# An own order for the head, the latent output and the handover to the experts, with a pool that is given up early

## The chip, the cores and the metric

The kernel runs on one core of a Trainium2 chip. The metric is the device time of one execution in microseconds (us). The engines are called as in the profile: PE (TensorE, matmul and transposes; PEld is its weight load), DVE (VectorE), ACT (ScalarE), POOL (GpSimd) and SP (SyncE, which issues most DMAs). Everything is in float32.

## What is computed

It is one decoder layer for 32 sequences of 256 tokens with 256 channels: causal self-attention with 16 heads on a shared latent of 72 numbers, cross-attention to 120 context rows, a mixture of 16 experts with a fixed capacity beside one shared expert, and a layernorm after each. Cut to what matters:

```python
Wdkv = x @ latent_w + latent_b                      # 72 columns, for all heads
q = einsum('btc,hcl->bhtl', x, Wd_w) + Wd_b
attn = softmax(causal(q @ Wdkv.T / sqrt(d_head)))
x = layernorm(x + reshape(attn @ Wdkv) @ out_w + out_b)
q, k, v = x @ Wq, ctx @ Wk, ctx @ Wv                # 16 heads of 64
x = layernorm(x + (softmax(q * depth**-0.5 @ k.T) @ v) @ Wo)
scores = softmax(x @ gate_w.T)                      # each expert takes its best 32 tokens of a sequence
flat = scatter_add(zeros, idx, (gelu(x_tok @ Wg) * (x_tok @ Wu)) @ Wd * score)
x = layernorm(x + flat + shared_expert(x))
```

## The kernel before, in words

The attention of a sequence n is cut into four quarters of four heads each. `attention_round(n)` (L795) runs them, each beginning with `scores(n, g)` (L401, called S0 to S3 here). Around them stands work of older sequences, so that PE always has something to do while a softmax is on its way: sequence n-1 gets its latent output and its cross queries, n-2 its cross softmax and output, n-3 is transposed and routed. `run` drops a step whose sequence doesn't exist, `both` runs a cross step for two column groups, `turns` the three transposes of a quarter.

The order within this section is written by hand for PE and ACT (`manual_schedule`). DVE, POOL and SP are ordered by the compiler's scheduler, which puts what stands under `urgent()` ahead; in the setup all engines go in program order, SP also in round 0. In the expert section PE and POOL are in program order.

The steps that matter here, with the names that the profile shows:

- `load` (L309) fetches x; `turn_x` (L320) transposes it (pxT, copied to xT on DVE, L174); `keys` (L327) projects to pk, from which ACT makes kT and DVE kD; `query_rest` (L361) and `queries` (L373) project the queries (pq) with wd_sb, a reordered copy of wd_w that `order_weights` (L254) makes: two DVE copies for the small rest (L266), one DVE copy `pack` for the first quarter (L260), the others on POOL, and scaled biases wdbs (L276).
- `scores` (L401) fills four PSUM banks (pS); DVE adds the mask and makes sm (L432). `weights` and `softmax` (L435, L442): DVE takes the maximum (nmax, L445), ACT the exponentials with their sums (L448), DVE the reciprocal (rs, L455), POOL the product (L456). `turn` (L458) transposes the result (pT) and copies it (pt, on ACT or DVE). `weigh` (pz, L490) and `weigh_rest` (pzr, L511) apply it.
- `latent_out` (L521): 36 matmuls to po, DVE adds the residual (r, L531), and `layernorm` (L143) makes x1: two statistics and two aggregates on DVE, an addition to rstd, its power -1/2 on POOL (L154), and two DVE instructions that write x1 (L156). `turn_x1` (L535) transposes x1 (px1T), copied on DVE (x1T).
- `cross_queries` (pqx), `cross_keys` (pkx), `cross_values` (pvx), `cross_scores` (pL), `cross_weights` (softmax to xsm_x), `cross_turn` (pxT at L623), `cross_weigh` (pc), `cross_out` (po at L653 and on, then layernorm 2); `turn_x2` (L671) transposes x2 (px2T).
- After round 31 comes `last_section` (L888). Then the self-attention pools are closed, and the expert pools take their place. `feed_forward` (L1062) is a generator of stretches; `fill(k)` (L1088) runs the next k, between which the last cross-attention steps are written by hand. `Expert.load` (L948) issues three weight loads on SP and four gathers on POOL (L958, xe), `turn` transposes the rows (px, L967), `gated` makes pg and pu, `down` pd and four scatters on POOL, which add into acc (L995).

PSUM has six banks for the tag r, and two for the tag l.

Of the kernel before, what the change touches and what calls it, by code (L numbers as in the profile page):

```python
# [26 lines left out]
P = 128  # L27
# [5 lines left out]
def decoder_kernel(  # L33
# [85 lines left out]
    nc.gpsimd.memset(mhalf, -0.5)  # L119

# [76 lines left out]
    ap = cross_pools.enter_context(tc.tile_pool(name="ca", bufs=2))  # L197
    self_pools = ExitStack()
# [5 lines left out]
    lat_sb = wp.tile([P, DC, LW], F32, name="lat_sb")  # L204
# [4 lines left out]
    wd_sb = wp.tile([P, DC, H * L], F32, name="wd_sb")  # L209
# [4 lines left out]
    wk_sb = cw.tile([P, DC, H * DH], F32, name="wk_sb")  # L214
    wv_sb = cw.tile([P, DC, H * DH], F32, name="wv_sb")
# [6 lines left out]
    kr = wp.tile([P, NG, T], F32, name="kr")  # L222
# [5 lines left out]

    def first_weights():


        raw = ow_sb.rearrange("p a b -> p (a b)").rearrange("p (c n) -> p c n", c=DC)
        nc.sync.dma_start(
            out=lat_sb[:, :, 0:L], in_=latent_w.rearrange("(c p) l -> p c l", p=P)
        )
        nc.sync.dma_start(out=raw, in_=wd_w.rearrange("(c p) n -> p c n", p=P))
        nc.scalar.dma_start(out=latb[0:L], in_=latent_b.unsqueeze(1))
        for j in range(1, HG):
            nc.scalar.dma_start(
                out=latb[LM + j * LR : LM + (j + 1) * LR], in_=latent_b[LM:].unsqueeze(1)  # L240
            )
        by_column = wd_b[LM:, :].rearrange("l (g j o) -> j (l g) o", j=HG, o=1)
        for j in range(HG):
            nc.sync.dma_start(
                out=wdbs[j * 32 : (j + 1) * 32, ZC - 1 : ZC], in_=by_column[j]
            )
        nc.vector.tensor_copy(
            lat_sb[:, :, L:].rearrange("p c (j l) -> p c j l", l=LR),
            lat_sb[:, :, LM:L].unsqueeze(2).to_broadcast([P, DC, HG - 1, LR]),
        )  # L250
        nc.scalar.dma_start(out=wdb_sb, in_=wd_b)
        nc.sync.dma_start(out=outb, in_=out_b.partition_broadcast(P))

    def order_weights():  # L254
        raw = ow_sb.rearrange("p a b -> p (a b)").rearrange("p (c n) -> p c n", c=DC)
        by_head = raw.rearrange("p c (h l) -> p c h l", l=L)

        def pack(copy, g):
            at = slice(2 * g * P, 2 * (g + 1) * P)
            copy(  # L260
                wd_sb[:, :, at].rearrange("p c (h l) -> p c h l", l=LM),
                by_head[:, :, g * HG : (g + 1) * HG, 0:LM],
            )

        for d in range(DC):
            nc.vector.tensor_copy(  # L266
                wd_sb[:, d, H * LM :].rearrange("p (j l g) -> p j l g", j=HG, l=LR),
                by_head[:, d, :, LM:].rearrange("p (g j) l -> p j l g", j=HG),
            )

        nc.vector.tensor_scalar(
            wdbs[:, ZC - 1 : ZC], wdbs[:, ZC - 1 : ZC], QSCALE, None, ALU.mult
        )
        pack(nc.vector.tensor_copy, 0)
        for odd in range(2):
            nc.vector.tensor_scalar(  # L276
                wdbs[odd * LM : (odd + 1) * LM, 0 : H // 2],
                wdb_sb[0:LM, :].rearrange("l (c two) -> l c two", two=2)[:, :, odd],
                QSCALE,
                None,  # L280
                ALU.mult,
            )
        for g in range(1, NG):
            pack(nc.gpsimd.tensor_copy, g)
# [510 lines left out]
    def attention_round(n):  # L795
        scores(n, 0)
        run(cross_scores, n - 2, 4, 0)
        run(cross_values, n - 1, 0)
        turns(n - 1, 3)
        both(cross_turn, n - 2, 0, 1)  # L800
        weights(n, 0, 0)
        queries(n, 1)
        run(turn_x2, n - 3)
        weights(n, 0, 1)
        run(weigh_rest, n - 1)
        run(weigh, n - 1, 2)
        run(weigh, n - 1, 3)
        if routed(n):
            route((n - 3) // BQ)
        run(cross_weigh, n - 2, 0)  # L810
        both(cross_weights, n - 2, 4, 0)
        run(latent_out, n - 1)
        if n:
            run(load, n + 1)
            run(load_context, n + 1)
        best_of(n, 1)

        scores(n, 1)
        run(cross_scores, n - 2, 4, 1)
        run(cross_values, n - 1, 1)  # L820
        turns(n, 0)
        both(cross_turn, n - 2, 4, 0)
        weights(n, 1, 0)
        cross_keys(n, 0)
        weights(n, 1, 1)
        run(turn_x1, n - 1)
        if n == 0:
            out_weights(0)
        if routed(n):
            score((n - 3) // BQ)  # L830
        queries(n, 2)
        run(cross_weights, n - 2, 4, 1, 0)
        run(cross_queries, n - 1, 0, 0)
        run(cross_weights, n - 2, 4, 1, 1)
        run(cross_queries, n - 1, 0, 2)
        best_of(n, 2)

        scores(n, 2)
        run(cross_scores, n - 1, 0, 0)
        run(cross_queries, n - 1, 4, 0)  # L840
        turns(n, 1)
        both(cross_turn, n - 2, 4, 1)
        weights(n, 2, 0)
        run(turn_x, n + 1)
        run(cross_queries, n - 1, 4, 2)
        weights(n, 2, 1)
        queries(n, 3)
        run(keys, n + 1)
        run(cross_weights, n - 1, 0, 0, 0)
        run(query_rest, n + 1)  # L850
        run(cross_weights, n - 1, 0, 0, 1)
        if n == 0:
            load_weights([(wv_sb, wv)])
            out_weights(1)
        best_of(n, 3)

        weigh(n, 0)
        weigh(n, 1)
        run(cross_weigh, n - 2, 4)
        scores(n, 3)  # L860
        run(cross_scores, n - 1, 0, 1)
        run(queries, n + 1, 0)
        turns(n, 2)
        run(place_keys, n + 1)
        both(cross_turn, n - 1, 0, 0)
        both(cross_weights, n - 1, 0, 1)
        cross_keys(n, 1)
        weights(n, 3, 0)
        run(values, n + 1)
        weights(n, 3, 1)  # L870
        run(cross_out, n - 2)
        if n == 0:
            load_weights([(wq_sb, wq), (wo_sb, wo), (gw_sb[:, :, 0:E], gate_w)])


        if n - 3 >= BG and (n - 3) % BG == 0:
            place((n - 3) // BG - 1)
        if n - 3 >= 0 and (n - 2) % BG == 0:
            select((n - 3) // BG)
# [8 lines left out]
    def last_section():  # L888

        cross_values(last, 0)  # L890
        both(cross_turn, last - 1, 0, 1)
        weigh(last, 2)
        turns(last, 3)
        turn_x2(last - 2)
        weigh(last, 3)
        weigh_rest(last)
        cross_weigh(last - 1, 0)
        cross_scores(last - 1, 4, 0)
        both(cross_weights, last - 1, 4, 0)
        latent_out(last)  # L900

    every = {getattr(mybir.EngineType, n) for n in ("PE", "SP", "DVE", "Activation", "Pool")}
    with tc.manual_schedule(engines=every):
# [6 lines left out]
        order_weights()  # L910
        query_rest(0)
        queries(0, 0)
# [5 lines left out]
    with tc.manual_schedule(engines={*by_hand, mybir.EngineType.SP}):  # L918
        attention_round(0)
    with tc.manual_schedule(engines=by_hand):  # L920
        for n in range(1, B):
            attention_round(n)
        last_section()
    self_pools.close()
# [3 lines left out]
    fw = expert_pools.enter_context(tc.tile_pool(name="fw", bufs=1))  # L928
    fp = expert_pools.enter_context(tc.tile_pool(name="fp", bufs=2))
    wsg_sb = fw.tile([P, DC, F], F32, name="wsg_sb")  # L930
    wsu_sb = fw.tile([P, DC, F], F32, name="wsu_sb")
    wsd_sb = fw.tile([P, FC, C], F32, name="wsd_sb")
# [3 lines left out]
    class Expert:  # L936
# [11 lines left out]
        def load(self):  # L948
            e = self.e
            self.wg = fp.tile([P, DC, F], F32, tag="wg", name=f"wg_{self.nm}")  # L950
            nc.sync.dma_start(out=self.wg, in_=wg[e].rearrange("(c p) f -> p c f", p=P))
            self.wu = fp.tile([P, DC, F], F32, tag="wu", name=f"wu_{self.nm}")
            nc.sync.dma_start(out=self.wu, in_=wu[e].rearrange("(c p) f -> p c f", p=P))
            self.wd = fp.tile([P, FC, C], F32, tag="wd", name=f"wd_{self.nm}")
            nc.sync.dma_start(out=self.wd, in_=wd[e].rearrange("(c p) d -> p c d", p=P))
            self.xe = fp.tile([P, NBK, XW], F32, tag="xe", bufs=3, name=f"xe_{self.nm}")
            for k, b in enumerate(self.blocks):
                nc.gpsimd.indirect_dma_start(  # L958
                    out=self.xe[:, k, :], out_offset=None, in_=xrows[b], in_offset=self.rows(b)
                )  # L960

# [41 lines left out]
    class Shared:  # L1003


        wg, wu, wd = wsg_sb, wsu_sb, wsd_sb

# [4 lines left out]
        def load(self):  # L1012
            if self.pair == 0:
                nc.sync.dma_start(out=wsg_sb, in_=ws_g.rearrange("(c p) f -> p c f", p=P))
                nc.sync.dma_start(out=wsu_sb, in_=ws_u.rearrange("(c p) f -> p c f", p=P))
                nc.sync.dma_start(out=wsd_sb, in_=ws_d.rearrange("(c p) d -> p c d", p=P))
            self.xT = fp.tile([P, DC, cols], F32, tag="xeT", bufs=3, name=f"fx2T_{self.nm}")
            nc.sync.dma_start(out=self.xT, in_=x2ts[self.pair].rearrange("p c i t -> p c (i t)"))

# [42 lines left out]
    def feed_forward():  # L1062
# [5 lines left out]
        units[0].load()  # L1068
        yield
        units[1].load()  # L1070
        units[0].turn()
        yield
        for u, unit in enumerate(units):
# [7 lines left out]
            if u + 2 < len(units):  # L1081
                units[u + 2].load()
            yield
# [8 lines left out]
    with tc.manual_schedule(engines={mybir.EngineType.PE, mybir.EngineType.Pool}):  # L1092
        fill(1)
        cross_values(last, 1)
        cross_scores(last - 1, 4, 1)
        both(cross_weights, last - 1, 4, 1)
        both(cross_turn, last - 1, 4, 0)
        turn_x1(last)
# [98 lines left out]
```

## Time and profile before

| | us |
|---|---|
| median of 3 runs | 3424.97 (3423.62 to 3425.28) |
| profiled execution | 3423.19 |
| its span | 3421.4 |
| busy: PE | 3386.6 |
| busy: DVE, ACT, POOL | 1549.0, 1491.7, 1071.0 |
| PE waiting for the two first causes: POOL's sm, the first x | 5.9, 4.0 |

The profiled execution is one of its own; its span lies between its first and last instruction. A row of the waits says: the engine and the instruction that waited, the engine and the instruction that released it, then the total, how often, and the longest. A row of a timeline says: start, length, engine, line of the code, operation, output and inputs with their shapes, how many in a row, and in brackets the idle time of the engine just before and what ended it. Matmuls overlap, so in a row of several the next may start before the listed end. The granted clock is the share of full speed that PE's clock had. "Steady" is a round in the middle of the first section.

### The profile page before, as it was taken

To read this page: it belongs to the slowest core of one execution; us is meant where nothing else is said; L and a number is where in the kernel's file an instruction comes from. 1 tells how busy PE (TensorE), PEld (TensorE's weight loads), DVE (VectorE), ACT (ScalarE), POOL (GpSimd) and SP (SyncE) were. 2 spreads that over 40 slices of the span, in tenths; PEclk is the share of its full clock that TensorE was granted. 3 is DMA by queue.
4 is the path that set the end of the run, shared out by engine and by line. 5 is a ranking of instruction groups with operands and counts; after the bars stand their busy time and mean duration, and the time that the engine had idled before them with its cause. 6 is when DMAs were issued, how large, how long until landed. Compare 5 with 4: busy or idle time off the path is not lost.

```text
span 3421.4 us, 60519 instructions
## 1 busy us (share of the span) xinstructions
PE 3386.6 (99%) x23516; PEld 2569.9 (75%) x23516; DVE 1549.0 (45%) x3416; ACT 1491.7 (44%) x5458; POOL 1071.0 (31%) x947
## 2 busy tenths in 40 slices
PE   8999999999999999999999999999999999999999
PEld 6888888888888888888888888886666655666555
DVE  4555455555555555545555645553322133222133
ACT  4555555555545655555555555554211111111111
POOL 3333323322323323223323232332444411444400
PEclk9999999999999999999999999999999999999999
DMA  3000000000000000000000000003455532455421
GB/s 98 9 17 23 20 22 17 18 18 23 20 21 18 18 17 23 21 20 19 17 18 17 24 20 21 16 12 100 104 125 125 132 91 59 117 125 124 106 84 50
DMA packets 142614, 164.58 MB, mean 48 GB/s; under 512 B 29432, under 2 KB 118264, under 8 KB 142328
## 3 DMA queue, kind: packets, MB, share of 16 engines
q1 hardware_dynamic: 117536, 126.08, 12.3%
q0 software_dynamic: 24576, 34.62, 5.7%
q8 instruction: 187, 3.06, 0.4%
q14 instruction: 99, 0.81, 0.1%
q10 hardware_dynamic: 216, 0.01, 0.0%
HBM read 105.61 MB, written 50.86 MB: 46 GB/s over the span
## 4 chain that ended last, share of the span: by engine, by line
PE 96%; DVE 2%; ACT 1%; POOL 1%; DMA 0%; issue 0%; SPq 0%; POOLq 0%; DVEq 0%
PE po L180 14%; PE pq L180 7%; PE pqx L180 7%; PE pu L180 6%; PE pd L180 6%; PE pg L180 6%; PE pS L423 5%; PE pz L490 5%; PE pT L470 5%; PE pc L639 3%; PE pkx L180 3%; PE pg_s L180 3%; PE pu_s L180 3%; PE pL L597 3%; PE pfo L180 3%; PE pxT L623 3%
## 5 line engine op out<-in xcount | busy, mean ns | idle before, releaser
L456 POOL TENSOR_TENSOR sm<-sm,rs 128x512 f32<-128x512 f32 (+1 forms) x256 | 375.2, 1466 | 675.6 <-DVE rs L455 624.8
L448 ACT ACTIVATE sm<-sm,nmax 128x128 f32<-128x128 f32 (+1 forms) x1024 | 453.0, 458 | 4.5 <-DVE nmax L445 4.3
L456 POOL TENSOR_TENSOR xsm_x<-xsm_x,rs_x 128x480 f32<-128x480 f32 x256 | 252.4, 986 | 610.9 <-DVE rs_x L455 609.9
L448 ACT ACTIVATE xsm_x<-pL,nmax_x 128x120 f32<-128x120 f32 x1024 | 353.4, 373 | 9.4 <-DVE nmax_x L445 9.4
L995 POOL DMA_INDIRECT acc<-eo,offs x128 | 200.8, 1568 | 322.3 <-DVE eo L992 292.9
L432 DVE TENSOR_TENSOR sm<-pS,mask 128x384 f32<-128x384 f32 x512 | 249.5, 548 | 77.0 <-PE pS L423 76.9
L180 PE MATMUL pq<-xT,wd_sb 128*128 128x256 f32 x1152 | 280.1, 384 | 2.6 <-DVE wd_sb L266 2.6
L566 ACT COPY vx<-pvx 120x512 f32<-120x512 f32 x64 | 37.5, 586 | 509.7 <-PE pvx L180 509.7
L180 PE MATMUL po<-ow_sb,zT 128*128 128x256 f32 x1152 | 257.2, 382 | 0.0
L180 PEld LDWEIGHTS po<-ow_sb,zT 128*128 128x128 f32 x1152 | 216.4, 190 | 39.8 <-DVE cxT L651 8.5
L180 PE MATMUL pu<-xeT,wu 128*128 128x512 f32 x512 | 242.1, 596 | 0.0
L180 PE MATMUL pqx<-x1T,wq_sb 128*128 128x256 f32 x1024 | 241.9, 385 | 0.0
L180 PE MATMUL pg<-xeT,wg 128*128 128x512 f32 x512 | 240.7, 593 | 0.0
L1059 DVE TENSOR_TENSOR hT<-gl,pu 128x512 f32<-128x512 f32 x128 | 87.9, 687 | 334.7 <-PE pu L180 254.6
L180 PEld LDWEIGHTS pq<-xT,wd_sb 128*128 128x128 f32 x1152 | 212.5, 191 | 33.1 <-DVE wd_sb L266 3.4
L445 DVE TENSOR_REDUCE nmax<-sm 128x4 f32<-128x512 f32 (+1 forms) x256 | 231.7, 946 | 3.2
L154 POOL TENSOR_TENSOR rstd<-rstd,mhalf 128x2 f32<-128x2 f32 (+1 forms) x97 | 67.1, 692 | 526.4 <-DVE rstd L153 526.4
L180 PE MATMUL po<-wo_sb,cxT 128*128 128x256 f32 x1024 | 227.6, 381 | 0.0
L180 PE MATMUL pd<-wd,hT 128*128 128x256 f32 x1024 | 226.3, 379 | 0.0
L448 ACT ACTIVATION_READ_ACCUMULATOR xsm_x<-pL,nmax_x 128x1 f32 x1024 | 226.0, 221 | 0.0
L180 PEld LDWEIGHTS pqx<-x1T,wq_sb 128*128 128x128 f32 x1024 | 191.3, 192 | 27.3
L180 PEld LDWEIGHTS pd<-wd,hT 128*128 128x128 f32 x1024 | 192.4, 190 | 25.6 <-issue 1.0
(136 smaller groups left out, 6211.7 us busy)
## 6 DMA issues: line engine op xcount, KB each, us to landing
wg<-in_wg_dram SPq DMA_DIRECT2D x32, 512.0 KB
wu<-in_wu_dram SPq DMA_DIRECT2D x32, 512.0 KB
wd<-in_wd_dram SPq DMA_DIRECT2D x32, 512.0 KB
x<-in_x_dram SPq DMA_DIRECT2D x32, 256.0 KB
rows<-x SPq DMA_DIRECT2D x32, 256.0 KB
acc<-x SPq DMA_DIRECT2D x32, 256.0 KB
x2t<-x2T SPq DMA_DIRECT2D x32, 256.0 KB
fx2T_s<-x2t SPq DMA_DIRECT2D x16, 512.0 KB
```

Source lines behind the costliest of these rows:

```text
L180: nc.tensor.matmul(acc, lhsT, rhs, start=(i == 0), stop=(i == n - 1))
L423: nc.tensor.matmul(pS[2 * a + odd][:, SEG[t]], st["qT", g][rows, a, t * P : (t + 1) * P], k[rows, 0 : (t + 1) * P], start=False, stop=(t = ...
L432: nc.vector.tensor_tensor(sm[:, j, :], pS[j], mask, ALU.add)
L445: nc.vector.tensor_reduce(nmax, src, AX.X, ALU.max, negate=True)
L448: nc.scalar.activation(dst[:, a, :], src[:, a, :], AF.Exp, bias=nmax[:, a : a + 1], accum_out=rs[:, a, :],)
L456: nc.gpsimd.tensor_tensor(dst, dst, rs.to_broadcast([P, n, width]), ALU.mult)
L470: nc.tensor.transpose(pT[:, j, :], block, ident)
L490: nc.tensor.matmul(pz[odd * LM : (odd + 1) * LM, a, k * P :], st["v"][:, k, 0:LM], moving(st, g, 2 * a + odd, k), start=(k == 0), stop=(k ...
L597: nc.tensor.matmul(pLs[odd][:, j, :], st["qxT", c0][rows, j, t * P : (t + 1) * P], st["kxT"][rows, c0 + j, :], start=True, stop=True,)
L623: nc.tensor.transpose(pT[:, j, :], st["xsm", c0, t, odd][:, j, :], ident)
L639: nc.tensor.matmul(pc[odd * DH : (odd + 1) * DH, a, :], st["vx"][:, 2 * (c0 + j0 + a) + odd, :], st["xpt", c0, odd][:, j0 + a, :], start=True,
L995: nc.gpsimd.indirect_dma_start(out=acc[b], out_offset=self.rows(b), in_=eo[:, k, :], in_offset=None, compute_op=ALU.add,)
```

## The change

1. **A pool for what only the scores and projections read.** lat_sb, wd_sb, wk_sb, wv_sb and kr move to a pool of their own, which is closed after the last scores. In its place a pool is opened for the first expert's and the second's gate and up weights (wg, wu) and gathered rows (xe). `Expert.load` is split into load, gather and load_down; the rest of the expert pools opens after the self-attention pools close, as before.
2. **An own order for the first half rounds.** wd_w comes in two loads, an early `Exp` on ACT (`warm`) is added, the biases wdbs and the first `pack` come before the copies for the rest, and the first queries before `query_rest(0)`. In round 0, x of sequence 1 is transposed and projected to keys within the first quarter, the rest of its queries and the transposes of quarter 0 follow S1.
3. **The latent output behind the second scores**, in all rounds: po of n-1 is put behind S1 and pL, the two cross softmaxes of quarter 0 before the first of the self-attention; behind po come pT, pxT, pq of quarter 2, pkx, px1T, pvx, pqx.
4. **An own order for the last half round** and the handover: `last_scores` and `last_weights` take the place of the second half of round 31 and of `last_section`, and stretches of the experts are put between their steps and the last cross-attention steps.

PE's instructions are the same in number. ACT gets one activation, SP one load more.

```diff
+    kp = score_pools.enter_context(tc.tile_pool(name="kw", bufs=1, side="right"))
...
-    lat_sb = wp.tile([P, DC, LW], F32, name="lat_sb")
+    lat_sb = kp.tile([P, DC, LW], F32, name="lat_sb")
...
-        nc.sync.dma_start(out=raw, in_=wd_w.rearrange("(c p) n -> p c n", p=P))
+        for part in (slice(0, HG * L), slice(HG * L, H * L)):
+            nc.sync.dma_start(out=raw[:, :, part], in_=by_part[:, :, part])
...
+        nc.scalar.dma_start(out=wdb_sb, in_=wd_b)
+
+        nc.scalar.activation(warm, mhalf[:, 0:1], AF.Exp)
...
-    def attention_round(n):
+    def first_half(n):
         scores(n, 0)
         run(cross_scores, n - 2, 4, 0)
         run(cross_values, n - 1, 0)
         turns(n - 1, 3)
         both(cross_turn, n - 2, 0, 1)
+        both(cross_weights, n - 2, 4, 0)
+        queries(n, 1)
+        if n == 0:
+            turn_x(1)
+            keys(1)
+        run(turn_x2, n - 3)
         weights(n, 0, 0)
-        queries(n, 1)
-        run(turn_x2, n - 3)
-        weights(n, 0, 1)
         run(weigh_rest, n - 1)
         run(weigh, n - 1, 2)
         run(weigh, n - 1, 3)
         if routed(n):
             route((n - 3) // BQ)
         run(cross_weigh, n - 2, 0)
-        both(cross_weights, n - 2, 4, 0)
+        weights(n, 0, 1)
+        best_of(n, 1)
+
+        scores(n, 1)
+        run(cross_scores, n - 2, 4, 1)
         run(latent_out, n - 1)
         if n:
             run(load, n + 1)
             run(load_context, n + 1)
-        best_of(n, 1)
-
-        scores(n, 1)
-        run(cross_scores, n - 2, 4, 1)
-        run(cross_values, n - 1, 1)
-        turns(n, 0)
+        else:
+            query_rest(1)
+            turns(0, 0)
+        weights(n, 1, 0)
+        weights(n, 1, 1)
+        if n:
+            turns(n, 0)
         both(cross_turn, n - 2, 4, 0)
-        weights(n, 1, 0)
+        queries(n, 2)
+        run(cross_weights, n - 2, 4, 1, 0)
         cross_keys(n, 0)
-        weights(n, 1, 1)
-        run(turn_x1, n - 1)
+        run(cross_weights, n - 2, 4, 1, 1)
...
+        run(turn_x1, n - 1)
+        run(cross_values, n - 1, 1)
         run(cross_queries, n - 1, 0, 0)
...
-    def last_section():
-
+    def last_scores():
+
+        scores(last, 2)
+        cross_scores(last - 1, 0, 0)
+        cross_queries(last - 1, 4, 0)
+        turns(last, 1)
+        both(cross_turn, last - 2, 4, 1)
+        weights(last, 2, 0)
+        cross_queries(last - 1, 4, 2)
+        weights(last, 2, 1)
+        queries(last, 3)
+        both(cross_weights, last - 1, 0, 0)
+        cross_keys(last, 1)
         cross_values(last, 0)
+        scores(last, 3)
+        cross_scores(last - 1, 0, 1)
+        cross_values(last, 1)
+
+    def last_weights():
+
+        both(cross_weights, last - 1, 0, 1)
+        weights(last, 3, 0)
+        turns(last, 2)
+        both(cross_turn, last - 1, 0, 0)
+        weights(last, 3, 1)
+        fill(1)
+        weigh(last, 0)
+        weigh(last, 1)
+        cross_weigh(last - 2, 4)
+        cross_out(last - 2)
+        cross_scores(last - 1, 4, 0)
         both(cross_turn, last - 1, 0, 1)
+        turns(last, 3)
+        both(cross_weights, last - 1, 4, 0)
+        fill(1)
+        turn_x2(last - 2)
         weigh(last, 2)
-        turns(last, 3)
-        turn_x2(last - 2)
         weigh(last, 3)
+        cross_weigh(last - 1, 0)
         weigh_rest(last)
-        cross_weigh(last - 1, 0)
-        cross_scores(last - 1, 4, 0)
-        both(cross_weights, last - 1, 4, 0)
         latent_out(last)
...
-        order_weights()
+        order_first()
+        queries(0, 0)
+        order_others()
         query_rest(0)
-        queries(0, 0)
...
+        first_half(last)
+        last_scores()
+    score_pools.close()
...
+    ep = expert_pools.enter_context(tc.tile_pool(name="fe", bufs=2, side="right"))
...
-        units[0].load()
+        for unit in units[0:2]:
+            unit.load()
         yield
-        units[1].load()
+        for unit in units[0:2]:
+            unit.gather()
+            yield
+        for unit in units[0:2]:
+            unit.load_down()
         units[0].turn()
         yield
...
+    with tc.manual_schedule(engines={*pinned, mybir.EngineType.Activation}):
         fill(1)
-        cross_values(last, 1)
+        last_weights()
+    self_pools.close()
...
+    with tc.manual_schedule(engines=pinned):
         cross_scores(last - 1, 4, 1)
         both(cross_weights, last - 1, 4, 1)
+        fill(1)
         both(cross_turn, last - 1, 4, 0)
+        fill(1)
         turn_x1(last)
         fill(1)
```

## The prediction, as it was put on record

> **What bounds the kernel now.** I read the page first (busy times, slices, chain), then the waits of TensorE (PE), then busy time by stretch, and last the timelines of PE and GpSimd (POOL) where a stretch fell short.
>
> ```profile
> PE 3386.6 (99%) x23516; PEld 2569.9 (75%) x23516; DVE 1549.0 (45%) x3416; ACT 1491.7 (44%) x5458; POOL 1071.0 (31%) x947
> PE   8999999999999999999999999999999999999999
> PE 96%; DVE 2%; ACT 1%; POOL 1%; DMA 0%; issue 0%; SPq 0%; POOLq 0%; DVEq 0%
> ```
>
> TensorE is the bound: 3386.6 of 3421.4 us busy, 96% of the chain that ended last. 34.8 us are idle, and that, with any matmul that ran at a lowered clock, is all that a change of order can win. The change alters no matmul. So the question is only which idle time goes, and which comes. The waits (total, times, longest, in us):
>
> ```profile
> PE pT L470 <- POOL sm L456: 5.9, 3, 2.3
> PE pxT L170 <- DMA x<-in_x_dram: 4.0, 1, 4.0
> PE pzr L511 <- DVE pt L474: 4.0, 3, 1.3
> PE px L967 <- DMA xe<-rows,offs: 3.1, 3, 1.4
> PE px1T L170 <- DVE x L156: 3.0, 1, 3.0
> PE pq L180 <- DVE wd_sb L266: 2.6, 1, 2.6
> PE pxT L623 <- POOL xsm_x L456: 2.0, 2, 1.7
> ```
>
> Nearly all occur once or thrice, not once a round. By stretches of 100 us PE is 100.00 busy from 120 to 2320, but for 98.67 to 98.68 in three rounds (pzr, 1.32 each). The rest is the head (first 120 us), the tail (about 7 us, untouched), and the place where attention hands over to the experts (columns: length; busy of PE, PEld, DVE, ACT, POOL; granted clock; DMA share, GB/s):
>
> ```profile
> 2320.00:2340.00 20.00, 20.00 (x186) 15.05 (x183) 7.19 (x17) 5.88 (x23) 2.14 (x3) 1.00 0.16 46
> 2340.00:2360.00 20.00, 13.91 (x66) 10.96 (x67) 4.90 (x11) 5.67 (x21) 10.49 (x11) 0.74 0.82 279
> 2400.00:2420.00 20.00, 18.00 (x75) 8.71 (x74) 5.77 (x11) 10.62 (x26) 10.76 (x10) 0.91 0.39 82
> ```
>
> The clock falls with the gaps. PE's timeline there, then POOL's:
>
> ```profile
> 2344.97 0.81 PE L170 MATMUL px1T<-ident,x 128*128 128x128 f32 x4 [2.95 <-DVE x L156]
> 2347.20 0.94 PE L967 MATMUL px<-ident,xe 128*128 128x128 f32 x2 [1.41 <-DMA xe<-rows,offs]
> 2351.44 9.24 PE L180 MATMUL pqx<-x1T,wq_sb 128*128 128x256 f32 x32
> ...
> 2412.03 0.65 PE L623 MATMUL pxT<-ident,xsm_x 128*120 128x128 f32 x4 [1.72 <-POOL xsm_x L456]
> ```
>
> ```profile
> 2339.83 1.21 POOL L958 DMA_INDIRECT xe<-rows,offs  x1 [4.60 <-DVE mv L152]
> 2341.35 0.97 POOL L958 DMA_INDIRECT xe<-rows,offs  x1 [0.30 <-issue]
> 2342.62 0.95 POOL L958 DMA_INDIRECT xe<-rows,offs  x1 [0.31 <-issue]
> 2343.59 0.73 POOL L154 TENSOR_TENSOR rstd<-rstd,mhalf 128x2 f32<-128x2 f32 x1
> ```
>
> Three gathers stand ahead of the small power instruction of the layernorm, so x1 of sequence 31 comes late. Then PE waits for the gathers themselves, because expert 0's rows and weights were asked for only after the self-attention pools closed. DMA is full there (350 to 371 GB/s).
>
> **The handover's loss, worked out.** From the end of pxT at 2342.02 to pL at 2360.61 are 18.59 us. At full clock the work is px1T 0.44 (steady rounds, start to start), eight px 0.95, pqx 2 x 3.55 = 7.10 (3.55 for sixteen at 1103.99): 8.49. Lost 10.1: four waits 2.95 + 1.41 + 0.92 + 0.79 = 6.1, and 4.0 by the clock (0.50 to 0.52 in 2348 to 2356). Second place: pg ends 2410.32, po starts 2420.62: 10.30 us for pxT 0.88, pu 1.72, pc 1.83, pg 1.72 = 6.15. Lost 4.15: waits 1.72 + 0.29, and 2.1 by the clock (0.73, then 0.84). Together 14.2 us.
>
> **The change, part by part.**
>
> *Early pool for the experts.* The SP and POOL instructions for experts 0 and 1 (four weight loads, eight gathers) move ahead by some 20 us. In the new order expert 0's gathers are past on POOL when the power instruction for x1 of 31 comes, and some 15 us of PE work (two pz pairs, pc, po2 and more) lie before px. The first two losses go: -10.1. Behind SP's queue nothing waits that PE needs soon. The copies of xeT now meet DVE work queued ahead (two max-reductions and an aggregate): about 0.4 at the first pg. The new order of the last half round brings px2T of sequence 29 close behind its layernorm: r 0.69, statistics 0.75 and 0.30, a cross max-reduction (1.21 for two) and a copy 0.68 ahead of rstd, the power 0.70, x 0.74. PE reaches px2T about 1.6 us before x2 is there: +1.6. The second place keeps its pattern: expert 0's four scatters (1.55 each, 0.30 between) and expert 2's four gathers (0.95 to 1.02) still stand on POOL ahead of the products of a cross softmax, now of sequence 31 (heads 4 on, second half). I take this wait at its own row, 2.0.
>
> *What the new gaps cost in clock* no row decides. The gap at 2412 (1.72 + 0.29) cost 2.1 more, while gaps of 2.35 at 26 us, 1.50 at 56 and 2.03 at 117 stand in stretches with a granted clock of 1.00. The Trainium skill, "TensorE: Matmul & The Clock Gate", Part 1, says that the clock halves only after an idle window of some 3.4 us. By that rule both new gaps are free of it: 1.6 + 0.4 + 2.0 = 4.0, gain 10.2. By the 2412 row both pay 2: 8.0, gain 6.2. The trace speaks against the rule at 2412, so I let the gap that keeps its place and pattern pay 2.1, and the px2T gap, nearest to the 1.50 at 56, nothing: 6.1, gain 14.2 - 6.1 = 8.1.
>
> *Latent output behind the second scores (31 rounds).* The 36 matmuls of po (7.97 us) move from before S1 to after it. Then, before px1T, PE has pT 1.30, pxT 0.88, pq 1.72, pkx 1.78 = 5.68 us, where it had 2.28 + 0.98 + 1.81 + 1.30 + 0.88 + 1.78 = 9.0. In that time x1 must come. Row by row from po's end: r 0.80, statistics to 1.6, one aggregate, the copy of pt to 2.3, the second aggregate, the copy of xpt to 3.1, rstd 3.25, power on POOL to 4.0, x (two) 4.8. Slack 0.9 us. Then pqx needs the copy of px1T on DVE; it stands behind a reciprocal that waits for an exponential group of ACT, some 6.2 after po, so it ends at about 7.0, and PE (pvx between) comes at 7.9. So 0 us, covered by pq and pkx. In return the second softmax has 8 us more cover, worth nothing where PE is already 100% busy. The bounds: it cannot gain, save the three pzr waits (4.0 at most, whose copy of pt I see unmoved: 0); it loses whatever the chain exceeds 5.68 by, times 31.
>
> *Head.* The Exp table load (1.28 us at 7.40, ahead of kT) is done earlier by the warm activation: but pk ends only at 7.91, so kT moves from 8.70 to about 7.95. On DVE kD (0.48) follows, the two bias scales (0.56 each) and pack 0 (0.70) come before the two 0.74 copies that pq waited for: 7.95 + 0.50 + 0.48 + 1.12 + 0.70 gives pq at about 10.8, not 10.52. The split weight load is one more SP instruction; whole, it had landed before 9.71, where DVE copies from it without a wait, and pack 0 reads it at 10.05. pq runs at the cold rate as before (633 ns a matmul against 378): S0 at about 15.6 instead of 15.27. Then turn_x(1), keys(1) fill PE where it waited 1.35 for qT and 2.35 for POOL; the price is a new wait at pk of sequence 1 of about 1.65, since xT's copy stands behind mask-adds (1.94) and max-reductions on DVE, and pT still waits some 2.5. By 56 us I count PE 0.5 ahead, bounds -1 and +1.5. The 4.0 for x stays, as do the 2.03 at 117 and the three pzr.
>
> **Sum.** 8.1 + 0 + 0.5 = 8.6. The profiled execution took 3423.19 (span 3421.4 and 1.8 around it), 1.8 under the median 3424.97. Against its own time 3414.6, on the median's footing 3416.4.
>
> **Rivals.**
> (a) Steady slack missing, slower. POOL works in order, and the product of the second half scores (1.89 us) stands directly ahead of the power instruction; on DVE its reciprocal stands ahead of r. If the exponentials come late, x1 does: 4.8 + 1.89 - 5.68 = 1.0 a round, 31 us, net +22: 3447. It decides once the wait passes 0.5 a round (31 x 0.5 = 15.5, less 8.6, is the 6.8 that make slower). For it: every round repeats it, and S1's softmax now starts with po and not after it. Against: from S1's end the exponentials need 0.9 + 1.81 + 1.55 + 1.97 = 6.2, po ends at 8.95. Chance 0.10, since the slack of 0.9 is of the size of my errors.
> (b) Gaps move: px2T, pg and pxT all meet the lowered clock and the head loses 1, or the place-round waits grow. Gain 0 to 6, about 3421. For it: the 2412 row, and DVE and POOL queues that are no shorter. Chance 0.22.
> (c) All of it is covered: expert fills hide x2 too, no clock is lost. Gain 11 to 16, about 3411. For it: 8 us of fill stand near each step; against: the POOL pattern at the second place is unchanged. Chance 0.20.
> The forecast, gain 6 to 11, has 0.48.
>
> **Numbers.** About 0.2%, 6.8 us, is what a measurement of this kernel can tell from no change: the line lies at 3418.2. Faster: 0.40 of the forecast's 0.48 and all of (c), 0.60. Slower: 0.09 of (a). Same: 0.31. The range leaves out (a) and the ends of (b) and (c): 3409 to 3422.5.
>
> **What would show it.** Right: no px1T or px among the waits, granted clock 1.00 from 2335 to 2360, rounds still 100.00 in 100, new waits of about 1.6 at px2T and of 2 at a pxT of L623 with a dip, pk of sequence 1 waiting 1.65, S0 near 15.6. Wrong: px1T waits in the list 31 times, or PE busy under 99 in the rounds; px waiting still (the gathers no earlier); clock dips at px2T; PE behind at 56 us.

## The result, and the profile after

The changed kernel takes 3411.41 us (median of 6 runs, 3410.86 to 3411.62) against 3424.05 for the kernel before beside it: ratio 0.9963, 95% interval 0.995 to 0.9976. That is 12.6 us faster, and 3411.41 lies inside the stated range. But 8.6 were forecast: 12.6 is above the forecast's own 6 to 11, in the band of rival (c), whose reason did not occur. The profiled execution's span is 3409.5 us, 11.9 less than before. That the sum came near is luck: it came out through two errors of opposite sign, and the larger part of this section is about them.

The page's row of busy times, and then PE's waits:

```profile
PE 3376.6 (99%) x23516; PEld 2568.9 (75%) x23516; DVE 1534.4 (45%) x3416; ACT 1501.9 (44%) x5461; POOL 1070.6 (31%) x947
```

```profile
PE pz L498 <- ACT pt L484: 1.3, 1, 1.3
PE pxT L631 <- POOL xsm_x L464: 1.3, 2, 1.0
PE po L181 <- ACT cxT L657: 1.0, 1, 1.0
PE px2T L171 <- DVE x L157: 0.9, 1, 0.9
PE pc L647 <- DVE zT L508: 0.8, 1, 0.8
PE pc L647 <- DVE cxT L659: 0.8, 1, 0.8
PE po L181 <- ACT vx L574: 0.7, 1, 0.7
```

px and px1T are gone from the list, as forecast. In their place stand six waits that the forecast did not have (pz, pc twice, po twice, and 0.4 at a pxT). PE's idle time hardly fell: 3409.5 - 3376.6 = 32.9 us against 34.8. What fell is its busy time, by 10 us for the same 23516 matmuls. Some of that is the clock, as the stretches of the handover show (columns as before):

```profile
2300.00:2320.00 20.00, 14.95 (x102) 11.04 (x100) 5.19 (x11) 9.51 (x39) 7.01 (x7) 1.00 0.33 113
2340.00:2360.00 20.00, 20.00 (x112) 14.33 (x111) 9.71 (x22) 10.53 (x35) 2.70 (x4) 1.00 0.40 132
```

The granted clock is 1.00 in both, as it is in the stretches up to 2420. The gap moved ahead, into 2300 to 2320, and cost no clock there.

To see where the time went I read the start of one instruction that has the same work ahead of it in both kernels: the first pzr of a sequence (that of sequence n stands in round n+1), and the first matmul of the shared expert's output (pfo) after the handover.

| | before | after | gained |
|---|---|---|---|
| pzr of sequence 0 | 58.76 | 58.49 | 0.27 (head) |
| pzr of sequence 30 | 2257.27 | 2251.22 | 6.05, so 5.78 in 30 rounds |
| first pfo | 2753.29 | 2741.17 | 12.12, so 6.07 in the handover |
| last pfo | 3407.14 | 3395.03 | 12.11 |

Head 0.3, rounds 5.8, handover 6.1. The forecast had 0.5, 0 and 8.1. A round gains 0.19 us although PE is 100.00 busy in it before and after. The PE timeline of round 14 shows how. The kernel before, po, and then from pL of the second scores on:

```profile
1011.46 8.04 PE L180 MATMUL po<-ow_sb,zT 128*128 128x256 f32 x36
...
1021.70 1.05 PE L597 MATMUL pL<-kxT,qxT 64*128 64x120 f32 x16
1022.68 1.98 PE L180 MATMUL pvx<-wv_sb,c 128*120 128x512 f32 x4
1024.50 1.47 PE L470 MATMUL pT<-ident,sm 128*128 128x128 f32 x12
```

The changed kernel in the same round, from po on, which now follows pL:

```profile
1011.95 8.04 PE L181 MATMUL po<-ow_sb,zT 128*128 128x256 f32 x36
1019.83 1.47 PE L478 MATMUL pT<-ident,sm 128*128 128x128 f32 x12
...
1026.17 1.88 PE L181 MATMUL pvx<-wv_sb,c 128*120 128x512 f32 x4
1027.89 3.62 PE L181 MATMUL pqx<-x1T,wq_sb 128*128 128x256 f32 x16
```

Read start to start, since a group's listed end overlaps the next. pvx behind pL takes 1024.50 - 1022.68 = 1.82; behind px1T 1027.89 - 1026.17 = 1.72. po behind pL takes 1019.83 - 1011.95 = 7.88; before, behind pc and ahead of the scores, it took 7.96 (1011.46 to 1019.42). 0.10 + 0.08 = 0.18 a round, nearly all of the 0.19. The shapes tell the groups apart: pL has weights of 64 rows by 128 columns (64*128), pc 120*64, pzr 128*32, which use a part of the array. po, pvx, pqx, pT use all of it. In the order before there were five places in a round where whole-array matmuls follow part-array ones, and five where it is the other way round; now there are four of each: pc, S1 and pL stand together.

Such a passage costs in both directions. In round 31 of the changed kernel pvx stands behind pkx, a whole-array group, and ahead of the fourth scores, which start at 2295.28:

```profile
2293.47 1.88 PE L181 MATMUL pvx<-wv_sb,c 128*120 128x512 f32 x4
```

It takes 1.81, 0.09 more than between two whole-array groups. Likewise the po of the cross output takes 7.05 ahead of scores (1061.04 to 1068.09 in the kernel before), but 6.95 in a round where transposes come next (765.18 to 772.13). These times repeat within 0.01 from round to round. So one passage is worth 0.09 to 0.10 us, and the two that went with po's old place, from pc to po and from po to S1, are the 0.19. Where pc and S1 now meet, both part-array, none is seen: in round 14 pc takes 1.88 and the scores 2.28 in both orders.

What happens at a passage to whole-array matmuls shows in the weight loads. First the kernel before, then the changed one:

```profile
1022.68 0.28 PEld L180 LDWEIGHTS pvx<-wv_sb,c 128*120 128x120 f32 x2
```

```profile
1026.06 0.29 PEld L181 LDWEIGHTS pvx<-wv_sb,c 128*120 128x120 f32 x2
```

Behind px1T the first load starts 0.11 us ahead of the first matmul (1026.17), under the transposes. Behind pL it starts with the matmul (1022.68), so about that much of it is laid open.

### The profile page after: what moved, and what is told of

The parts are those of the page before. It is cut to its first block, busy times and chain, and to the rows that moved or that the text cites. A ratio compares the mean times of both kernels' runs of the same rounds, so it can differ in the third digit from the quotient of the medians.

```text
span 3409.5 us, 60236 instructions
## 1 busy us (share of the span) xinstructions
PE 3376.6 (99%) x23516; PEld 2568.9 (75%) x23516; DVE 1534.4 (45%) x3416; ACT 1501.9 (44%) x5461; POOL 1070.6 (31%) x947
## 4 chain that ended last, share of the span: by engine, by line
PE 97%; DVE 1%; ACT 1%; POOL 0%; DMA 0%; issue 0%; SPq 0%; POOLq 0%; ACTq 0%
PE po L181 14%; PE pq L181 7%; PE pqx L181 7%; PE pd L181 6%; PE pg L181 6%; PE pu L181 6%; PE pS L431 5%; PE pz L498 5%; PE pT L478 5%; PE pc L647 3%; PE pkx L181 3%; PE pu_s L181 3%; PE pg_s L181 3%; PE pL L605 3%; PE pxT L631 3%; PE pfo L181 3%
## 5 line engine op out<-in xcount | busy, mean ns | idle before, releaser
L463 DVE RECIPROCAL rs<-rs 128x4 f32<-128x4 f32 x256 | 45.4, 177 | 378.3 <-ACT sm L456 375.8
L456 ACT ACTIVATION_READ_ACCUMULATOR sm<-sm,nmax 128x1 f32 x1024 | 213.1, 208 | 0.0
L181 PEld LDWEIGHTS po<-wo_sb,cxT 128*128 128x128 f32 x1024 | 192.0, 190 | 27.4 <-ACT cxT L657 1.4
```

The lines of the kernel that those rows point to most:

```text
L181: nc.tensor.matmul(acc, lhsT, rhs, start=(i == 0), stop=(i == n - 1))
L456: nc.scalar.activation(dst[:, a, :], src[:, a, :], AF.Exp, bias=nmax[:, a : a + 1], accum_out=rs[:, a, :],)
```

## The experiments

Theory A: a round gains because one passage from part-array to whole-array matmuls goes (and one back with it, though the expectations below count both as one), and the handover by the early gathers. Rivals: B, the rounds give nothing; C, po behind pc waited unseen for the copies of zT. The time of each run below stands beside the kernel before on the same chip.

**The rounds alone.**

```diff
-    def attention_round(n):
+    def attention_round(n):   # kernel before
+        (later_half if n else first_half)(n)   # later_half: the changed first half
+        second_half(n)
```

> The kernel before with only the new first half of rounds 1 to 31 (latent output behind the second scores); head, second half and handover as before. Theory A (in each round one passage fewer from matmuls that use part of the array to matmuls that use all of it, about 0.2 us each): pzr comes every 72.95 us instead of 73.15, the handover begins 5.8 us sooner, time about 5.5 to 6 us below the kernel before. Rival B (the rounds give nothing, as the prediction had it, and all of the gain lies in the handover and the head): within 1.5 us of the kernel before.

3416.27 us against 3424.33: ratio 0.9978 (0.9969 to 0.9987), 8.1 less. B falls. The profile has pzr of sequence 0 at 58.51 and of sequence 30 at 2252.90: 2194.39 apart, 4.12 less than before, though the clock was halved once at the wait of 2.03 us near 117 (for 3.4 us, so 1.7 us). Without it the rounds gain 5.8: from sequence 4 to sequence 8 pzr takes 293.19 us, as in the changed kernel, and 293.96 before. The rest of the 8.1 is clock again: in the handover, whose order is that of before, it was halved for 6.8 us in this profile and not for 13.7.

**The handover alone.**

```diff
-    def first_half(n):    # changed kernel: first half, second half and setup
+    def first_half(n):    # those of the kernel before
```

> The changed kernel with the rounds and the head of before, so only the early pool and the new order of the last half round and the handover. Theory A: the handover is worth 5.9 us of the profiled 11.9, so about 5.5 to 6.5 below before. Rival B: nearly the whole gain, 11 to 12.5 below.

3421.05 against 3424.33: ratio 0.9991 (0.9983 to 0.9999), 3.3 less, where A had expected 5.5 to 6.5. The waits are those of the changed kernel. But now these gaps, here between 2307 and 2323, did cost the clock:

```profile
2308.00:2312.00 4.00, 2.53 (x18) 1.81 (x20) 0.43 (x3) 2.53 (x11) 2.93 (x3) 0.82 0.98 355
2312.00:2316.00 4.00, 3.21 (x28) 2.20 (x26) 0.69 (x1) 0.00 (x0) 0.00 (x0) 0.75 0.35 133
```

(0.18 + 0.25) x 4 / 0.5 = 3.4 us at half clock, 1.7 us lost. And pzr of sequence 31, 2.74 us in the profile of the changed kernel, took 4.93 (2337.01 to 2341.94), with breaks that are put down to nothing the profile shows ("issue"): 2.2 more. From pzr of 30 to the first pfo the profile takes 494.10 us against 496.02 before. With the two losses taken off, its gain of 1.9 becomes 5.8, as in the changed kernel; that is a subtraction, and no run showed it.

**The head alone.** Setup and round 0 of the changed kernel, all else as before.

> The kernel before with only the new head (setup and round 0). Both theories: pzr of round 0 comes about 0.3 us sooner, so 0 to 0.5 below before, not to be told from it. If the head were worth 2 us or more, the sum of parts would have to be drawn up anew.

3423.17 against 3424.33: ratio 0.9998 (0.999 to 1.0007), no difference that can be told. pzr of sequence 0 ("of round 0" in the expectation) starts at 58.93. In the four profiles with the head of before it starts at 57.92 to 59.20, in eight with the new head at 58.31 to 59.24, and in a ninth, with a halving of the clock at 29, at 60.55. So the 0.3 of the first table is within what one head varies. The three medians (8.1, 3.3 and 1.2) add up to the whole 12.6, but that is chance too, for each holds its own losses of clock.

**One passage put back.**

```diff
         scores(n, 0)
         run(cross_scores, n - 2, 4, 0)
-        run(cross_values, n - 1, 0)
...
         weights(n, 0, 1)
+        run(cross_values, n - 1, 0)
         best_of(n, 1)
         scores(n, 1)
```

> The changed kernel, with the cross values of n-1 (pvx, four whole-array matmuls) moved from behind pL of the first scores to between pc and the second scores. Nothing is left out. Theory A (passages from part-array to whole-array matmuls): pc is followed by whole-array matmuls again, so the round gets one passage back at that place while pT, also whole-array, now follows pL: 0.1 to 0.2 us a round, 3 to 6 us slower than the changed kernel. Rival C (po behind pc waited unseen for the copies of zT, and this wait is what went): the round stays at 72.95, the time within 1.5 us of the changed kernel.

3429.04 against 3424.33 (ratio 1.0013, 1.0006 to 1.0019): 17.6 above the changed kernel, more than either theory had. PE's timeline where pvx now stands:

```profile
1013.45 1.95 PE L647 MATMUL pc<-xpt,vx 120*64 120x256 f32 x16
1015.33 1.98 PE L181 MATMUL pvx<-wv_sb,c 128*120 128x512 f32 x4
```

The next scores start at 1017.24, so pvx took 1.91 between pc and the scores, 0.19 more than between whole-array groups: two passages. Behind pL and ahead of pT it took 1.81, so the move costs it 0.09 or 0.10. pT behind pL takes 1.37 instead of 1.31. Round 14 as a whole is 0.22 longer, 6.6 in 30 rounds. About 0.15 of the 0.22 is at these two passages, as A has it; the remaining 0.07 is at pq ahead of px2T (1.80 instead of 1.73), where no passage is, and its cause is open. C falls: pvx reads no zT, and pays behind pc all the same. The profile's span is 15.7 us above that of the changed kernel. Of the 9 that the rounds do not explain, the clock at 119 took 1.7 and pzr of sequence 31 2.2 (4.90 us, with an "issue" break). The last 5 stand in the first two rounds and in the three with routing, where the transposes have lost the cover of pvx: 8.5 against 5.1 us of waits for POOL's sm, and 3.4 of new ones for DVE; the 4.3 that pzr waited are gone in return. So the move did not test the passage alone.

**A passage taken away, as I thought.**

```diff
         run(cross_weigh, n - 2, 4)
+        run(values, n + 1)
         scores(n, 3)
...
         weights(n, 3, 0)
-        run(values, n + 1)
```

> The changed kernel, with the values of n+1 (pv, two small transposes of 72 rows) moved from ahead of the cross output po to ahead of the fourth scores, so that they stand in a run of part-array matmuls. Theory A: the passage from pv to po goes, po takes 6.90 instead of 7.05 us, 0.10 to 0.15 a round, 3 to 4.5 us faster than the changed kernel. Rival C (unseen waits for copies, not passages): within 1 us of it.

3418.16 against 3423.93 (ratio 0.9984, 0.9977 to 0.9991), 6.7 slower than the changed kernel, not 3 to 4.5 faster. PE's timeline:

```profile
1051.32 0.34 PE L357 MATMUL pv<-ident,kT 72*128 72x72 f32 x2
```

po now takes 7.01 (1060.65 to 1067.66) instead of 7.05, but pv 0.28 (to 1051.60) instead of 0.13. With its 72 rows, more than 64, it behaves as a whole-array group, and between pc and the scores it makes two passages more. 0.15 - 0.04 = 0.11 a round, and the profile's 30 rounds are 3.7 longer. My sorting of pv was wrong, and the miss fits the theory with pv on the other side; that reading was made after the run. Another 2.2 us is pzr of 31 again, 4.87 us with "issue" breaks.

**The gathers late.**

```diff
-        for unit in units[0:2]:
-            unit.gather()
-            yield
+        yield
+        yield
+        for unit in units[0:2]:
+            unit.gather()
         for unit in units[0:2]:
             unit.load_down()
```

> The changed kernel, with the eight gathers of experts 0 and 1 issued only when expert 0 is turned, the weights as early as in the change. If the early gathers are what removed the waits of the handover: px waits for its rows again, 5 us or more, the granted clock falls below 1 there, 5 to 12 us slower than the changed kernel. If the new order of steps alone did it: within 1.5 us.

3426.05 against 3423.93 (ratio 1.0007, 1.0001 to 1.0014), 14.6 above the changed kernel. PE's timeline:

```profile
2351.63 1.03 PE L1022 MATMUL px<-ident,xe 128*128 128x128 f32 x2 [9.72 <-DMA xe<-rows,offs]
```

With two shorter ones behind it (0.48 and 0.82) 11.0 us idle, and the clock halved for 13.7. With the new order of steps and early weights, but late rows, the handover is worse than before (504.42 us from pzr of 30 to the first pfo against 496.02): the early gathers are what pays. What the early weights are worth, this run does not show.

**The new waits of the handover.** ScalarE's timeline of the changed kernel shows what they are:

```profile
2303.95 1.09 ACT L484 COPY pt<-pT 128x512 f32<-128x512 f32 x2
2311.25 1.07 ACT L574 COPY vx<-pvx 120x512 f32<-120x512 f32 x2 [6.22 <-PE pc L647]
...
2315.13 0.60 ACT L657 COPY cxT<-pc 128x512 f32<-128x512 f32 x1
```

The values of 31 go into a buffer (two in turn) that those of 29 hold until pc of 29 is done. ScalarE stood 6.22 us before that copy, and xpt, the exponentials, zT and cxT queued behind it: cxT, which po waits for, came at 2315.13. The wait of 1.34 at pz lies ahead of that, in the same queue: pt was copied at 2303.95 only, behind the exponentials of a cross softmax and of the first scores (from 2299.71). The edit moves both.

```diff
     def last_weights():
+        cross_weigh(last - 2, 4)
+        turns(last, 2)
+        both(cross_turn, last - 1, 0, 0)
         both(cross_weights, last - 1, 0, 1)
         weights(last, 3, 0)
-        turns(last, 2)
-        both(cross_turn, last - 1, 0, 0)
         weights(last, 3, 1)
...
-        cross_weigh(last - 2, 4)
```

> The changed kernel, with pc of sequence 29 put ahead of the last transposes, and the two softmaxes behind these on ScalarE. In the changed kernel ScalarE's copies of the last cross values can start only when pc of 29 has freed their buffer, and six copies queue behind them; PE waits 0.38, 1.34, 0.80, 0.80, 0.71 and 1.04 us between 2302 and 2316. If that queue is the cause: most of this goes, 3 to 5 us faster than the changed kernel. If those waits come from PSUM banks or from softmax latency: within 1 us.

3410.74 against 3423.93: ratio 0.9964 (0.995 to 0.9977), within 1 us of the changed kernel. All six waits are gone. That points to ScalarE's queue; the edit also moves pc ahead on PE, so for the two waits of pc, which are listed for copies on DVE, it is argued and not shown apart. But PE came sooner to px2T of 29, and met its layernorm:

```profile
PE px2T L171 <- DVE x L157: 2.5, 1, 2.5
```

2.5 instead of 0.9, and that gap cost the clock (halved for 3.4 us at 2322). From pzr of 30 to the first pfo it is 1.2 us shorter than the changed kernel. The median does not tell the two apart: the changed kernel itself came out at 3411.41 and, in the last experiment, at 3413.40.

**Both edits together.**

> The two edits together: values ahead of the fourth scores, and pc of 29 ahead of the last transposes. If both causes are right they add: 6 to 9 us faster than the changed kernel. If neither: within 1 us.

3414.45 against 3423.93 (ratio 0.9975, 0.9965 to 0.9985), 3.0 above the changed kernel and not 6 to 9 below: the loss of the values edit (3.7 us in this profile's 30 rounds as well) on top of the small gain of the other.

**px2T moved too.** The edit to the handover, and turn_x2(last - 2) put behind cross_weigh(last - 1, 0), beside the changed kernel itself.

> The changed kernel with pc of 29 ahead of the last transposes and the two softmaxes behind these (as in the run before), and the transpose of x2 of sequence 29 put behind the remaining weigh steps and pc of 30, so that its layernorm has some 7 us of matmuls more. In that run px2T waited 2.5 us and the clock was halved for 3.41 us. If the waits of the handover can be covered by order alone: no wait at px2T, no drop, 4 to 6 us faster than the changed kernel. If they only move on: within 1.5 us of it, with a new wait of 2 us or more between 2300 and 2345.

> The changed kernel itself, on the same chip, beside the last experiment: 3411.4 by all theories, for the difference between the two.

3410.01 and 3413.40 against 3424.19 (ratios 0.9958, 0.9944 to 0.9971, and 0.9971, 0.9959 to 0.9982): 3.4 us faster than the changed kernel on the same chip, the best version here, short of the 4 to 6 expected. px2T no longer waits; a wait of 1.9 at pz took part of it, listed as ended by a reciprocal of a cross softmax:

```profile
2323.42 1.52 PE L498 MATMUL pz<-pt,v 128*64 128x256 f32 x16 [1.92 <-DVE rs_x L463]
```

From pzr of 30 to the first pfo it is 3.3 us shorter than the first profile of the changed kernel. The second profile of the changed kernel shows how much one kernel varies: span 3414.1 instead of 3409.5, with one halving at the gap near 117 (1.7 us), and pzr of 31 at 4.92 us with an "issue" break of 0.83 (2.2 us). By this second measurement the change is worth 10.8 us.

**What a gap costs in clock.** The prediction could not decide this, so I measured it by itself, in one execution of the kernel before with a stall in each of the rounds 4 to 27.

```diff
+    def stall(n):
+        first = bank("r", [P, P], f"gap0_{n}")
+        nc.tensor.transpose(first, gap[:, 0:P], ident)
+        nc.scalar.copy(gap[:, 0:P], first)
+        for k in range(n % 6):
+            nc.scalar.copy(gap, gap)
+        second = bank("r", [P, P], f"gap1_{n}")
+        nc.tensor.transpose(second, gap[:, 0:P], ident)
```

> The kernel before, with one stall of PE in each of the rounds 4 to 27, behind the latent output: a transpose, then 1 to 6 copies on ScalarE in a chain, then a transpose of the result. The output is unchanged. The gaps grow from about 1 us (round number divisible by 6) to about 4 us (remainder 5), at 24 different phases. The clock rule (halved only after an idle window of 3.4 us): no drop below 3.4 us. The row at 2412 of the kernel before (1.72 + 0.29 us idle, clock halved for one stretch): gaps of 2 us cost a drop in some rounds, and the share of rounds with a drop grows with the gap.

| idle time listed, us | 0.36 | 1.00 | 1.66 | 2.31 | 2.95 | 3.60 |
|---|---|---|---|---|---|---|
| rounds with a drop, of 4 | 0 | 0 | 0 | 2 | 4 | 4 |

The drops of this profile start a whole number of 3.413 us apart: those at 288.31, 366.82 and 670.60, for example, are 23 and 89 times 3.413 apart. So the clock is set by the windows of a fixed grid, wherever a gap begins, and the grid can be laid over every profile, for each has a drop, if only at its end (3406.60 in that of the changed kernel). Two gaps of 2.31 us, the first cut by the grid (1130.45 to 1132.76, no drop), the second nearly whole in one window (2052.81 to 2055.12, drop):

```profile
1131.40:1134.81 3.41, 2.06 (x27) 1.75 (x29) 1.58 (x7) 1.24 (x3) 0.69 (x1) 1.00 0.25 82
2053.00:2056.41 3.41, 1.29 (x19) 1.03 (x21) 2.31 (x8) 1.97 (x4) 0.69 (x1) 1.00 0.29 77
2056.42:2059.82 3.40, 3.40 (x26) 3.08 (x28) 1.77 (x4) 0.00 (x0) 0.00 (x0) 0.50 0.00 0
```

In the first case PE is idle for 1.35 us of the window shown and 0.95 of the one before, in the second for 2.12, and the next window runs at half clock, which costs at most 1.7 us of work. Two of the drops at 3.60 lasted two windows. Counted so over all thirteen profiles, for windows at full clock: 2.03 us or more of listed idle time in one window was followed by a drop in 21 of 21 cases, 1.67 to 1.92 us in 4 of 14, and 1.66 us or less in none (93 of these had 1.0 us or more). So the clock falls well below 3.4 us of idle time, and several short gaps count together: in the run of the handover alone 0.45 and 1.34 us fell into one window (1.78), with a drop, while in the changed kernel no window of the same waits held more than 1.50. That it lost no clock there is luck of the grid. The gap of 2.03 us near 117 likewise lost clock in some profiles (2.04 in one window) and none in others (1.59 and 0.43).

In the kernel before, the drops are (0.30 + 0.50 + 0.48) x 4 / 0.5 = 10.2 us, three windows, and (0.27 + 0.16) x 4 / 0.5 = 3.4, one window, behind 1.88 us of idle time in one.

## Why the prediction was right, and where it was not

*px and px1T go, with their clock.* Right: -10.1 forecast, both waits gone, clock 1.00. The run with late gathers brings px's wait back (11.0 us), and not px1T's.

*The second place keeps its pattern.* Right in pattern (four scatters and four gathers ahead of the cross products on POOL), wrong in size: 1.0 + 0.29 of wait instead of 2.0, and no clock instead of 2.1. 1.29 us in one window costs no clock; the step took the 2.01 of before as a price of the place, when it was a price of the idle time in one window. A drop of one window costs 1.7 at most, so 0.4 of the 2.1 was something else; the 6.15 of that sum left out the passages.

*px2T 1.6 and pg 0.4.* 0.86 and none.

*Handover as a whole, 8.1.* It gave 6.1. The term that was missing is the 5.1 us of six new waits (0.38, 1.34, 0.80, 0.80, 0.71 and 1.04), most of them tied to ScalarE's queue. I had followed DVE's and POOL's queues through the new order and not ScalarE's, where a copy with a buffer to wait for held up all that stood behind it. Their removal gained only 1.2, since px2T then waited 1.6 us more and the clock fell once (1.7).

*"It cannot gain" in the rounds, "worth nothing where PE is already 100% busy".* This step failed: the rounds gave 5.8 us, nearly half of the whole. A PE row at 100% still holds time in which no matmul gets ahead: the passages between part-array and whole-array groups, 0.09 to 0.10 us each, two of them fewer in each round. The Trainium skill has the rule that I missed, "TensorEngine Tiling (Array Packing)", Key Properties: changing the tiling mode drains the engine. No price is given there. The traces agree where one of the two groups is whole-array, in both directions; from pc to the scores, also a change of shape, they show none. The steady slack, on the other hand, was right: in round 14 x1 was ready 4.6 us after po (r at 1020.03 to x at 1024.43, forecast 4.8), and px1T came after 5.9; px1T is not in the list of waits.

*Head 0.5.* 0.3 in the profile, not to be told from nothing, and the other profiles show no gain either. pk waited 1.5 (forecast 1.65). S0 began at 15.21, not 15.6: DVE's scales took 0.34 together and pack 0.43, where I had taken 1.12 and 0.70 from rows in which they ran beside POOL's packs (11.01 to 12.97).

*The clock rule.* By the rule (a whole idle window of some 3.4 us; the Trainium skill, "TensorE: Matmul & The Clock Gate", Part 1) the sum would have been 10.2 for the handover, by the row 6.2. Neither decides, and that 6.1 came out near the row's sum is chance: no clock was lost, and the new waits took its place. The length of a drop and the fixed grid agree with that page's free-running window of 3413 ns; the idle time that sets a drop off does not, since 2.03 us or more in a window always did it here, and 1.67 once.

*The rivals.* (a), the steady wait, did not occur; (b) occurred in part (waits at px2T and a pxT, no clock), and in the run of the handover alone with a drop; (c) did not, since 7.2 us of waits remained.

What stays open: why pzr of 31 took up to 2.2 us longer in some profiles and not in others ("issue" names no cause; loads of about 100 GB/s are under way there, but in the first profile of the changed kernel, without a break, as well), what decides between 1.67 and 1.92 us of idle time in a window, and the 0.07 at pq in the run with one passage put back.

## What to carry to other kernels

A timeline of a busy TensorE is to be read start to start, group by group: where the same group takes longer behind one neighbour than behind another, the order is worth time though no wait is listed. Keep part-array matmuls together, and count the passages to whole-array ones and back. When work is moved, follow every in-order queue it passes, ScalarE's too, and ask of each copy which buffer it must wait for. Keep TensorE's idle time in any 3.4 us below about 1.7 us, short gaps added up: from 2.0 us in a window on, each case here cost up to another 1.7.

## What the runs showed of the hardware that I had not expected

- A passage between matmuls with 32- or 64-row or 32- or 64-column weights and whole-array ones costs 0.09 to 0.10 us in either direction (pvx 1.72 us with none, 1.81 or 1.82 with one, 1.91 with two), and 0.06 for transposes behind pL. Behind pL the weight load starts with its matmul and not 0.11 us ahead of it. Between two part-array shapes some such time is seen at one place (pz takes 2.75 us ahead of pg, 2.65 ahead of pc) and none at another (pc and the scores). The transposes pv of 72 rows behave as whole-array ones (0.28 us between pc and the scores, 0.13 between whole-array groups).
- The clock is halved for 3.413 us or a multiple, on a fixed grid of 3.413 us, behind a window of it with 2.03 us or more of idle time (21 of 21), with 1.67 to 1.92 us in 4 of 14 cases, and never with 1.66 or less.
- One kernel's profiles differ by up to 4.6 us (3409.5 and 3414.1), by one such drop at a gap of 2.03 us (1.7 us), and by a matmul group that ran 2.2 us longer without a listed cause.
